# Two adjacency layers on one core: turning x and its weights with VectorE, moving leaky slopes to ScalarE and residual sums to GpSimd, and giving loads other queues

## The chip, the core and the metric

The kernel runs on one core of one Trainium2 chip. The core has TensorE (matrix products, shown as PE, with its weight loads as PEld), VectorE (DVE), ScalarE (ACT), GpSimd (POOL) and SyncE (SP), which here only issues transfers. SP, ACT and POOL each have a DMA queue of their own, and all queues share 16 DMA engines. The metric is the device time of one launch in microseconds (us). Before the change the median of three runs is 1766.97 us (1764.3 to 1770.71).

## The reference, cut to what is computed

The input x is 4096 x 512 (float32), adj is 4096 x 4096 (0 or 1, about 32 ones in a row).

```python
# layer 0
keep   = Ab & (cumsum(Ab, axis=1) <= 64)          # the first 64 neighbours of a row
cnt    = keep.sum(axis=1)
xj     = leaky_relu((keep @ X) / max(cnt, 1) @ W_nb.T + b_nb)     # slope 0.01
xi     = leaky_relu(X @ W_line.T + b_line)
x1     = layernorm(X + xi + where(cnt > 0, xj, 0))
# layer 1
Wh     = x1 @ W + bW
e      = leaky(Wh @ a1 + b1 + (Wh @ a2 + b2).T, 0.2); e = where(adj > 0, e, -9e15)
out    = layernorm(x1 + softmax(e, axis=1) @ Wh)
```

## The kernel before, in words

The 4096 rows are cut into 32 blocks of 128 rows (`NB`); a row block of x is 128 partitions by 512 columns (`C`). The product with W_nb is pulled in front of the aggregation: the kernel keeps Y = X @ W_nb.T in two halves (`y_hi`, `y_lo`, lines 344 and 373) and later multiplies the 0/1 map by both. There are four stages, each a Python loop whose order of calls is the order of the instructions on every engine; nothing reorders them.

**Stage 1, linear maps (loop at line 332).** For every block i TensorE makes two products of 4 x 2 matmul records (`linear`, line 288), with W_nb and with W_line. Both operands need the contraction on the partitions, so x and the weights must be turned first. `transpose_to` (lines 112 to 117) does this on TensorE: four 128 x 128 transposes into PSUM and one ScalarE copy out. `turn_x(i + 1)` stands at the head of iteration i. `own` (lines 317 to 322) is three VectorE operations (add the bias, `max(0.01 t, t)`, add x) and a store of `xi + x` to DRAM on the GpSimd queue. x is loaded once (`load_x`, line 238), on the ACT queue two blocks ahead. `fold_w` (line 300, at i = 2) works out W a1 and W a2 with ten VectorE operations.

**Flag chunks.** Beside the products the kernel turns adj into one byte per edge. A row block has two chunks of 2048 columns, 64 in all. `codes_until(s)` runs chunks until s of them are scanned; for each it issues `load_adj` (1 MB, SP queue, line 152), `edge` (ScalarE, line 158), `scan` (VectorE: a running count at line 169, a copy at 173, a product at 174, and for every fourth chunk five small operations, lines 182 to 186), and `pack` (ScalarE copy, line 192, store on the GpSimd queue, line 193). Tiles for chunks exist twice, so a load waits for the `edge` two chunks back. Before the change 22 chunks are made in stage 1.

**Stage 2, aggregation (loop at line 420).** For each block, 64 matmuls (line 433) add the map times `y_hi` and `y_lo`. The map comes back from DRAM turned by a DMA transpose (`load_kt`, line 387, two blocks ahead, SP queue) and is opened by ScalarE (`make_kt`, line 221). `finish(i - 1, g)` (line 389) finishes the block before in four pieces: scale, bias and leaky slope (394, 397), residual sum and statistics (401, 121 to 127; the power at line 127 runs on GpSimd), layer norm and store (132, 408), and two sums for the attention scores (413). The other 42 chunks are made here, 1.5 to a block.

**Stage 3, Wh = x1 @ W (loop at line 656).** x1 is loaded in squares of 32 partitions (`load_turned`, line 473, four transfers to a block, ACT queue, three blocks ahead), so that one VectorE instruction (line 491) that turns 32 x 32 squares turns the whole block. `load_ct(0)` (line 502) fetches four turned code blocks on the SP queue at i = 6. `greatest` (line 516, i = 12 to 19) takes the row maxima, with a ScalarE piece (523), a VectorE piece (527) and the next `load_nat` on SP. `shifts(0)` (line 534, i = 22) writes a small tile to DRAM and reads it back spread over the partitions (544, 546, SP queue).

**Stage 4, attention (loop at line 681).** `produce` makes the weights on ScalarE and VectorE, `consume` multiplies them by Wh (line 601).

Of the kernel before, what the change touches and what calls it, by code (L numbers as in the profile page):

```python
# [20 lines left out]
P = 128  # L21
SQ = 32
NEIGHBORS = 64.0
EPS = 1e-5

# [6 lines left out]
def two_layer_adj_gnn(  # L32
# [56 lines left out]
    bias_nb = const.tile([P, C], F32, name="bias_nb")  # L89

    wa = const.tile([P, 2, NC], F32, name="wa")
    wa_row = const.tile([P, 2, C], F32, name="wa_row")
# [45 lines left out]
    with ExitStack() as l0:  # L138
# [88 lines left out]
        with ExitStack() as la:  # L227
            wp = la.enter_context(tc.tile_pool(name="l0_w", bufs=1))
            work = la.enter_context(tc.tile_pool(name="l0_work", bufs=2))

            bias_line = wp.tile([P, C], F32, name="bias_line")
            w_t = {}
            xbs, xts, pys, pls = {}, {}, {}, {}

            def load_x(i):
                if i < NB:
                    xbs[i] = work.tile([P, C], F32, name="xb", bufs=4)
                    (nc.sync if i < 3 else nc.scalar).dma_start(xbs[i], x_blk(i))

            def turn_x(i):  # L240
                if i < NB:
                    xts[i] = work.tile([P, NC, P], F32, name="xt")
                    transpose_to(xts[i], lambda k: xbs[i][:, ts(k, P)], NC)
# [8 lines left out]
            for name in ("nb", "line"):  # L252
                t = early("a")
                raw[name] = [t[:, c, :] for c in range(NC)]
# [9 lines left out]
            def load_w(name, src, queues):  # L264
                for c in range(NC):
                    queues[c % len(queues)].dma_start(raw[name][c], src[ts(c, P), :])
# [7 lines left out]
            def turn_w(name, idle=0):  # L274

                wt = wp.tile([P, NC, C], F32, name=f"wt_{name}")
                for c in range(NC):
                    if idle:
                        spin(idle)
                    transpose_to(  # L280
                        wt[:, :, ts(c, P)], lambda k: raw[name][c][:, ts(k, P)], NC
                    )
# [28 lines left out]
            def spread_wa():  # L311
                nc.sync.dma_start(
# [4 lines left out]
            def own(i):  # L317
                t = work.tile([P, C], F32, name="t")
                nc.vector.tensor_tensor(t, pls.pop(i), bias_line, ALU.add)  # L319
                nc.vector.scalar_tensor_tensor(t, t, 0.01, t, ALU.mult, ALU.max)  # L320
                nc.vector.tensor_tensor(t, t, xbs.pop(i), ALU.add)
                nc.gpsimd.dma_start(own_d[i], t)

            load_x(0)
            load_w("nb", w_nb, (nc.scalar, nc.sync))
            load_x(1)
            load_w("line", w_line, (nc.sync,))
            load_x(2)
            spin(12)
            turn_x(0)  # L330
            turn_w("nb", 2)
            for i in range(NB):
                if i == 0:
                    nc.sync.dma_start(bias_line, b_line.partition_broadcast(P))
                if i > 0:
                    turn_x(i + 1)
                xt = xts.pop(i)
                pys[i] = linear(xt, "nb")
                if i == 0:
                    turn_w("line")  # L340
                pls[i] = linear(xt, "line")
                if i == 0:
                    turn_x(1)
                nc.scalar.copy(y_hi[:, i, :], pys[i])
                if i > 0:
                    own(i - 1)
                if i > 0:
                    load_x(i + 2)
                if i == 0:
                    load_w("w", w, (nc.sync,))  # L350
                if i == 1:
                    load_rows()
                    nc.gpsimd.dma_start(bias_nb, b_nb.partition_broadcast(P))
                if i == 2:
                    fold_w()
                if i == 3:
                    spread_wa()
                if i > 3:
                    codes_until(int((i - 3) * 22 / (NB - 6)) if i < NB - 3 else 22)
# [16 lines left out]
            own(NB - 1)  # L376
# [4 lines left out]
        RATE = 1.5  # L381
        start = done[0]

        def load_kt(b):
            if b < NB:
                ktbs[b] = ktb_p.tile([P, NT, P], BF16, name="ktb")
                nc.sync.dma_start_transpose(ktbs[b], code_d[b])

        def finish(i, g):
            if i < 0:  # L390
                return
            if g == 0:
# [4 lines left out]
                nc.vector.scalar_tensor_tensor(t, t, 0.01, t, ALU.mult, ALU.max)  # L397
                fin[i] = t
            elif g == 1:
                t, y = fin[i], owns.pop(i)  # L400
                nc.vector.scalar_tensor_tensor(
                    y, t, some[:, i : i + 1], y, ALU.mult, ALU.add
                )
# [365 lines left out]
```

## Time and profile before

The profiled execution took 1767.0 us, and its span (first to last instruction) is 1764.9 us; the other 2.1 us lie around it. It stands within 0.1 us of the median of the runs.

| stretch of the span, us | stage | PE busy, us | DVE busy, us | ACT busy, us |
|---|---|---|---|---|
| 0 to 67 | 1, start | 55.5 | 20.8 | 13.7 |
| 67 to 192 | 1 | 118.6 | 119.9 | 70.3 |
| 192 to 272 | 1, end | 77.6 | 78.0 | 42.2 |
| 272 to 736 | 2 | 464.0 | 407.1 | 297.2 |
| 736 to 870 | 3 | 118.0 | 86.2 | 25.8 |
| 870 to 1765 | 4 | 886.3 | 690.2 | 426.1 |

Busy time says that an engine had an instruction in it, not that the instruction ran at its best rate: matmuls are pipelined, and one that starts late can still be counted as busy. The chain of work that ended last, and the order of time of each engine, say which engine the others waited for. A queue name (SPq, ACTq) is time in which an engine's issuing part was busy or waited.

### The profile page before, as it was taken

What the parts mean: (1) busy time and instruction counts of PE and PEld (TensorE: products, weight loads), DVE (VectorE), ACT (ScalarE), POOL (GpSimd) and SP (SyncE); (2) the same over time, 40 slices, a digit from 0 to 9 for tenths busy, and PEclk for the clock granted to TensorE, in tenths of its full rate; (3) what the DMA queues carried; (4) which work ended last, traced back from release to release, by engine and by line L of the source; (5) the groups of instructions that cost most, each with busy time, mean ns of one, the idle gap of its engine ahead of it and who ended that gap; (6) DMA issues with size and microseconds to landing.
All of it is one profiled execution on the core that took longest, in us unless ns stands there. A gap on an engine that the chain in (4) does not pass through costs nothing.

```text
span 1764.9 us, 14748 instructions
## 1 busy us (share of the span) xinstructions
PE 1720.0 (97%) x5118; PEld 949.6 (54%) x5118; DVE 1402.2 (79%) x1649; ACT 875.3 (50%) x910; POOL 192.9 (11%) x234
## 2 busy tenths in 40 slices
PE   8799999999999999989899999999999999999998
PEld 5344447888888888733344444444444444444443
DVE  3599998999999997458677986968869689696754
ACT  2355555767667674112355463644636445364331
POOL 1011112223232322100000100001000010000100
PEclk9899999999999999999999999999999999999999
DMA  4566667676767673762402304122041220411100
GB/s 143 191 220 204 205 222 204 192 221 198 221 203 210 207 204 95 133 148 79 100 25 55 88 24 96 60 64 68 24 95 56 65 68 27 96 50 46 48 0 25
DMA packets 209227, 206.57 MB, mean 117 GB/s; under 512 B 154848, under 2 KB 170240, under 8 KB 200832
## 3 DMA queue, kind: packets, MB, share of 16 engines
q1 hardware_dynamic: 174352, 145.55, 30.8%
q0 software_dynamic: 13056, 44.07, 6.6%
q10 hardware_dynamic: 21744, 16.00, 3.4%
q8 instruction: 41, 0.67, 0.2%
q14 instruction: 34, 0.28, 0.1%
HBM read 130.02 MB, written 42.00 MB: 97 GB/s over the span
## 4 chain that ended last, share of the span: by engine, by line
PE 84%; DVE 8%; DMA 5%; issue 1%; SPq 1%; ACT 1%; ACTq 0%; POOLq 0%; DVEq 0%
PE acc L601 49%; PE acc L433 26%; PE acc L288 5%; DVE left L169 3%; PE acc L661 2%; DMA xb<-in_x_dram 2%; DMA ct<-code_d 1%; SPq L506 1%; PE pt L116 1%; DMA x1b<-x_d 1%; DVE pen L527 1%; DVE t L320 1%; DVE y_lo L373 1%; DMA uv_d<-uv 1%; DVE t L319 1%
## 5 line engine op out<-in xcount | busy, mean ns | idle before, releaser
L601 PE MATMUL acc<-wh,p 128*128 128x512 f32 x2048 | 881.2, 592 | 0.0
L601 PEld LDWEIGHTS acc<-wh,p 128*128 128x128 f32 x2048 | 388.5, 190 | 486.0 <-issue 485.3
L433 PE MATMUL acc<-y_lo,kt 128*128 128x512 f32 x1016 | 395.2, 389 | 0.0
L433 PE MATMUL acc<-y_hi,kt 128*128 128x512 f32 x1016 | 395.2, 389 | 0.0
L561 ACT ACTIVATE p<-row,e 128x512 f32<-128x512 f32 x256 | 182.8, 714 | 419.1 <-PE acc L601 367.4
L564 DVE TENSOR_TENSOR p<-p,p 128x1024 f32<-128x1024 f32 x128 | 156.2, 1221 | 124.7 <-ACT p L561 124.6
L127 POOL TENSOR_TENSOR rs<-ve,neg_half 128x1 f32<-128x1 f32 x64 | 101.5, 1587 | 1152.1 <-DVE ve L125 1152.1
L221 ACT ACTIVATE kt<-ktb,steep 128x1024 fp32r<-128x1024 uint8 x124 | 142.8, 1152 | 154.2 <-PE acc L433 154.2
L433 PEld LDWEIGHTS acc<-y_hi,kt 128*128 128x128 f32 x1016 | 190.8, 188 | 39.5
L433 PEld LDWEIGHTS acc<-y_lo,kt 128*128 128x128 f32 x1016 | 190.8, 188 | 39.5
L561 ACT ACTIVATE p<-row,e_fifth 128x512 f32<-128x512 f32 x256 | 180.8, 706 | 1.4 <-DVE p L564 1.3
L566 DVE TENSOR_TENSOR p<-p,ct 128x1024 f32<-128x1024 f32 x128 | 156.8, 1225 | 4.4
L523 ACT ACTIVATE pen<-nat,far 128x2048 bf16<-128x2048 uint8 x64 | 127.3, 1990 | 63.4 <-DMA x1b<-x_d 52.1
L571 DVE TENSOR_TENSOR zacc<-zacc,p 128x1024 f32<-128x1024 f32 x120 | 147.0, 1225 | 4.1
L169 DVE TENSOR_TENSOR_SCAN left<-two,edge 128x2048 bf16<-128x2048 f32 x32 | 141.4, 4417 | 6.4 <-ACT edge L158 6.4
L169 DVE TENSOR_TENSOR_SCAN left<-two,ends,edge 128x2048 bf16<-128x2048 f32 x32 | 143.3, 4478 | 0.0
L158 ACT ACTIVATE edge<-a,steep 128x2048 bf16<-128x2048 int32 x64 | 127.5, 1993 | 17.8 <-DVE left L174 10.5
L661 PE MATMUL acc<-ws,x_t 128*128 128x512 f32 x256 | 116.0, 611 | 16.0 <-DVE x_t L491 15.8
L192 ACT CAST code<-left 128x2048 uint8<-128x2048 bf16 x64 | 120.5, 1883 | 0.8 <-DVE left L174 0.8
L288 PE MATMUL acc<-wt_nb,xt 128*128 128x512 f32 x256 | 119.2, 610 | 0.9 <-ACT wt_nb L117 0.7
L288 PE MATMUL acc<-wt_line,xt 128*128 128x512 f32 x256 | 115.2, 592 | 0.7 <-ACT wt_line L117 0.7
L661 PEld LDWEIGHTS acc<-ws,x_t 128*128 128x128 f32 x256 | 49.1, 195 | 82.4 <-issue 57.0
(103 smaller groups left out, 1029.1 us busy)
## 6 DMA issues: line engine op xcount, KB each, us to landing
a<-in_adj_dram SPq DMA_DIRECT2D x64, 1024.0 KB, 5.5
code_d<-code POOLq DMA_DIRECT2D x64, 256.0 KB, 4.4
nat<-code_d SPq DMA_DIRECT2D x32, 512.0 KB, 3.6
own_d<-t POOLq DMA_DIRECT2D x32, 256.0 KB, 4.3
own<-own_d SPq DMA_DIRECT2D x32, 256.0 KB, 2.8
x_d<-own POOLq DMA_DIRECT2D x32, 256.0 KB, 3.4
x1b<-x_d SPq DMA_DIRECT2D x32, 256.0 KB, 5.5
x1b<-x_d ACTq DMA_DIRECT2D x120, 64.0 KB, 2.1
```

Source lines behind the costliest of these rows:

```text
L158: nc.scalar.activation(edge_of[s], loaded.pop(s), AF.Sigmoid, bias=steep[:, 0:1], scale=STEEP)
L169: nc.vector.tensor_tensor_scan(left, two.to_broadcast([P, CH]), e, NEIGHBORS + 2.0 if h == 0 else end, ALU.max, ALU.subtract,)
L221: nc.scalar.activation(kts[s], bytes_.rearrange("p t (i r) -> p t r i", r=2), AF.Sigmoid, bias=steep[:, 1:2], scale=STEEP,)
L288: nc.tensor.matmul(pl, lhs_t[:, k, :], w_t[name][:, k, :], start=(k == 0), stop=(k == NC - 1),)
L433: nc.tensor.matmul(accs[i], kt[:, k // 2, k % 2, :], term[:, j, :], start=(j == 0 and term is y_hi), stop=(j == NB - 1 and term is y_lo),)
L523: nc.scalar.activation(pen, nats[b].bitcast(U8)[:, ts(h, HALF)], AF.Relu, bias=far, scale=-FAR)
L561: nc.scalar.activation(dst[:, r, :], uvs[g][:, k, :], AF.Exp, bias=e[:, b : b + 1])
L564: nc.vector.tensor_tensor(p0, p0, p1, ALU.max)
L566: nc.vector.tensor_tensor(p0, p0, code.rearrange("p (x r) -> p r x", r=2), ALU.min)
L571: nc.vector.tensor_tensor(zaccs[g], zaccs[g], p0, ALU.add)
L601: nc.tensor.matmul(accs1[g][k], p_[:, r, ts(k, P)], wh[:, 2 * t_ + r, :], start=(t_ == 0 and r == 0), stop=(t_ == NT - 1 and r == 1),)
L661: nc.tensor.matmul(pw, x1t[:, k, :], ws[:, k, :], start=(k == 0), stop=(k == NC - 1))
```

## The change

- **x and the layer-0 weights are turned by VectorE.** They are loaded in squares (`squares`: four transfers of 64 KB to a block of x, eight of 128 KB to a weight), and `turn` is one VectorE transpose to a block of x and four to a weight. The TensorE transposes and the ScalarE copies of stage 1 go. The opening run of idle TensorE transposes (`spin`) grows from 12 (and 8 between weights) to 40.
- **x is loaded twice.** The squares come on the SP queue, three blocks ahead, into a constant tile `late` that later holds the bias and the attention rows. The plain copy for the residual sum comes on the GpSimd queue (`load_own_x`).
- **Leaky slopes go to ScalarE** (`AF.Prelu`) in stages 1 and 2; in stage 2 the factor `some` is applied there too. **Residual sums go to GpSimd** (`tensor_tensor` add).
- **20 chunks** are made in stage 1, and 44 in stage 2 at 25/16 to a block.
- **`finish`** has its sums (old line 413) one block later, and the statistics one piece later.
- **Stage 3:** `load_turned` moves from the ACT to the SP queue; `load_ct(0)` is issued one transfer at a time at i = 8, 11, 14 and 17. The bias and the spread rows come late, on the GpSimd queue (`load_late`).

```diff
+            AHEAD = 20
...
+            def squares(dst, src):
+                return [
+                    (dst[ts(n, SQ)], src[:, ts(n, P)].rearrange("(j a) c -> a j c", a=SQ))
+                    for n in range(NC)
+                ]
-            def load_x(i):
...
-                    (nc.sync if i < 3 else nc.scalar).dma_start(xbs[i], x_blk(i))
+            def load_turned_x(i):
+                if i < NB:
+                    xrs[i] = late[:, i % 3, :].rearrange("p (j c) -> p j c", c=P)
+                    for dst, src in squares(xrs[i], x_blk(i)):
+                        nc.sync.dma_start(dst, src)
+            def load_own_x(i):
+                xbs[i] = work.tile([P, C], F32, name="xb", bufs=4)
+                nc.gpsimd.dma_start(xbs[i], x_blk(i))
+            def turn(dst, src):
+                nc.vector.transpose(
+                    dst.rearrange("p m (j a) -> p j m a", a=SQ),
+                    src.rearrange("p j (m b) -> p j m b", b=SQ),
+                )
             def turn_x(i):
...
-                    transpose_to(xts[i], lambda k: xbs[i][:, ts(k, P)], NC)
+                    turn(xts[i], xrs.pop(i))
...
-            def own(i):
+            def own_line(i):
                 t = work.tile([P, C], F32, name="t")
                 nc.vector.tensor_tensor(t, pls.pop(i), bias_line, ALU.add)
-                nc.vector.scalar_tensor_tensor(t, t, 0.01, t, ALU.mult, ALU.max)
-                nc.vector.tensor_tensor(t, t, xbs.pop(i), ALU.add)
-                nc.gpsimd.dma_start(own_d[i], t)
+                return t
+            def own(i, t):
+                nc.scalar.activation(t, t, AF.Prelu, alpha=SLOPE)
+                y = xbs.pop(i)
+                nc.gpsimd.tensor_tensor(y, y, t, ALU.add)
+                nc.gpsimd.dma_start(own_d[i], y)
...
+            for k in (0, 1, 2, 3, 4, 5):
+                nc.scalar.dma_start(*nb_parts[k])
+            load_turned_x(0)
+            for k in (6, 7):
+                nc.sync.dma_start(*nb_parts[k])
+            load_turned_x(1)
+            for part in parts_of("line", w_line):
+                nc.sync.dma_start(*part)
+            load_turned_x(2)
+            spin(40)
             turn_x(0)
-            turn_w("nb", 2)
+            turn_w("nb")
+            turn_x(1)
+            turn_w("line")
             for i in range(NB):
...
+                load_turned_x(i + 3)
                 if i > 0:
                     turn_x(i + 1)
                 xt = xts.pop(i)
                 pys[i] = linear(xt, "nb")
                 pls[i] = linear(xt, "line")
                 nc.scalar.copy(y_hi[:, i, :], pys[i])
                 if i > 0:
-                    own(i - 1)
+                    t = own_line(i - 1)
...
                 if i == 2:
                     fold_w()
                 if i > 3:
-                    codes_until(int((i - 3) * 22 / (NB - 6)) if i < NB - 3 else 22)
+                    codes_until(min((i - 3) * AHEAD // (NB - 6), AHEAD))
...
                     y_lo[:, i, :], pys.pop(i), y_hi[:, i, :].bitcast(F32), ALU.subtract
                )
+                if i > 0:
+                    own(i - 1, t)
+                load_own_x(i)
+                if i == 1:
+                    load_rows()
+                if i == NB - 2:
+                    load_late()
...
-        RATE = 1.5
+        RATE = 25 / 16
         def finish(i, g):
+            if g == 0 and i > 0:
+                y, _ = fin.pop(i - 1)
+                for k in range(2):
...
+                        accum_out=e12[:, k, i - 1 : i],
             if g == 0:
...
-                nc.vector.scalar_tensor_tensor(t, t, 0.01, t, ALU.mult, ALU.max)
+                nc.scalar.activation(t, t, AF.Prelu, alpha=SLOPE, scale=some[:, i : i + 1])
             elif g == 1:
-                nc.vector.scalar_tensor_tensor(y, t, some[:, i : i + 1], y, ALU.mult, ALU.add)
+                nc.gpsimd.tensor_tensor(y, y, t, ALU.add)
+            elif g == 2:
                 fin[i] = y, ln_stats(y)
...
-                nc.scalar.dma_start(
+                nc.sync.dma_start(
...
-        if i == 6:
-            load_ct(0)
+        if i in range(8, 8 + 3 * GB, 3):
+            load_ct(0, (i - 8) // 3)
```

## The prediction, made before the changed kernel was run

> **What bounds the kernel now.** I read the page first: the busy times and the chain of work that ended last.
>
> ```profile
> PE 1720.0 (97%) x5118; PEld 949.6 (54%) x5118; DVE 1402.2 (79%) x1649; ACT 875.3 (50%) x910; POOL 192.9 (11%) x234
> PE acc L601 49%; PE acc L433 26%; PE acc L288 5%; DVE left L169 3%; PE acc L661 2%; DMA xb<-in_x_dram 2%; DMA ct<-code_d 1%; SPq L506 1%; PE pt L116 1%; DMA x1b<-x_d 1%; DVE pen L527 1%; DVE t L320 1%; DVE y_lo L373 1%; DMA uv_d<-uv 1%; DVE t L319 1%
> ```
>
> TensorE carries 84% of the chain, but the lines L433 and L601 (stages 2 and 4) hold nearly all of it. L288, the products of stage 1, has 5%, and VectorE lines stand beside it. So I asked for the busy times stage by stage (columns: stretch, its length, then busy us of PE, PEld, DVE, ACT, POOL, the granted clock, DMA share, GB/s):
>
> ```profile
> 67.00:192.00 125.00, 118.62 (x318) 54.11 (x317) 119.88 (x115) 70.25 (x60) 15.16 (x28) 0.99 0.64 214
> 272.00:736.00 464.00, 464.00 (x2049) 384.32 (x2048) 407.09 (x525) 297.19 (x211) 115.27 (x106) 1.00 0.67 193
> 736.00:790.00 54.00, 48.55 (x116) 21.30 (x115) 28.13 (x50) 5.08 (x4) 2.90 (x4) 0.97 0.79 160
> 830.00:870.00 40.00, 31.58 (x70) 13.51 (x69) 19.10 (x28) 8.74 (x14) 0.00 (x0) 0.91 0.53 110
> 870.00:1765.00 895.00, 886.33 (x2113) 395.85 (x2111) 690.24 (x752) 426.10 (x557) 42.44 (x60) 1.00 0.20 53
> ```
>
> In stage 1 (67 to 192) VectorE is busy 96%; stage 2 is solid TensorE; stage 3 has holes in every engine; stage 4 is TensorE again. The order of time on VectorE shows what one block of stage 1 costs:
>
> ```profile
> 84.07 0.68 DVE L373 TENSOR_TENSOR y_lo<-acc,y_hi 128x512 fp32r<-128x512 f32 x1
> 84.67 0.68 DVE L319 TENSOR_TENSOR t<-acc,bias_line 128x512 f32<-128x512 f32 x1
> 85.38 0.69 DVE L320 SCALAR_TENSOR_TENSOR t<-t 128x512 f32<-128x512 f32 x1
> 86.11 0.69 DVE L321 TENSOR_TENSOR t<-t,xb 128x512 f32<-128x512 f32 x1
> 86.72 4.42 DVE L169 TENSOR_TENSOR_SCAN left<-two,edge 128x2048 bf16<-128x2048 f32 x1
> ...
> 91.36 1.23 DVE L174 TENSOR_TENSOR left<-edge,left 128x2048 bf16<-128x2048 bf16 x1
> 92.50 0.69 DVE L373 TENSOR_TENSOR y_lo<-acc,y_hi 128x512 fp32r<-128x512 f32 x1
> ```
>
> From start to start: y_lo 0.60, bias 0.71, slope 0.73, sum 0.61, chunk 5.78, in all 8.43 us a block, while the two products take TensorE 6.87 (their groups start at 261.56, 264.99 and 268.42). VectorE sets the pace. The chain in order of time shows the holes of stage 3, which runs from 737.4 to 869.15, 131.8 us for 32 x 3.43 = 109.9 of products, so 21.9 are lost:
>
> ```profile
> 745.08 11.87 DMA ct<-code_d
> 757.81 6.71 DMA x1b<-x_d
> ...
> 829.01 9.22 DMA uv_d<-uv
> ...
> 847.54 5.73 DMA ct<-code_d
> ```
>
> Loads of x1 wait behind four DMA transposes at 742 to 765 and again at 838 to 858. I put the loss at 6.3 us for the first (idle 3.8 before 755.17, then 10.2 us for 18 records worth 7.7), 10.7 for the second (27.9 us from 841.25 for five blocks of 3.43) and the rest, 4.9, at `greatest`, where VectorE needs 4.18 a block.
>
> **Stage 1, the steps.** *Start.* Before, block 1 begins at 22.03. Now the 40 idle transposes end at 10.8 at the rate of the first twelve (2.82 us for 12), or about 8 at the later rate (0.60 for four). SP issues 4 + 2 + 4 + 8 + 4 transfers at some 0.44 each (the median of L474, the same form): x0 is out by 2.5, line's weights by 8.9; ACT's six parts of nb by 3.4. With 4 to 5 us to landing (nb now: 4.6 to 4.9) and four transposes of 0.71 (L491), the first product starts near 10; line's weights are turned near 14.5, and block 1 starts near 18.0: 4 us earlier.
>
> *VectorE per block.* Slope (0.73) and sum (0.61) go, a turn comes at 0.71 (L491, 709 ns, the same shape). A block has 0.71 + 0.71 + 0.60 = 2.02, with a chunk 7.80. The formula puts 20 chunks in blocks 5 to 29: 25 x 2.02 + 20 x 5.78 + 5 x 0.9 (the small operations) = 170.6, against 25 x 6.87 = 171.8 on TensorE. They balance, and single blocks may be late: a turn may start when TensorE ends block i - 1 (two `xt` tiles) and is needed one block later, so 6.87 - 0.71, about 6 us, are free. The old TensorE transposes (0.43 a block) and copies (0.58 on ACT) go. Two chunks (11.6) move to stage 2.
>
> *ScalarE.* y_hi 0.59, edge 1.99, pack 1.88 and the slope, taken as an ACTIVATE of 128x512 (L561, 0.71): 5.2 us a block, under 6.87. It is behind edge and pack; who waits for it is GpSimd's add alone. Relu (L523) ran after Sigmoid in stage 3 without a table load, so I take none for Prelu.
>
> *GpSimd.* The add has no row. Bounds: 0.3 us (a one-input 128x128 operation at the start, 0.295) and 4.67 (the power L127 beside a scan); four times 0.295, 1.18, is nearest in size and is my value. What it does to VectorE is the open cost:
>
> ```profile
> L127 POOL TENSOR_TENSOR rs<-ve,neg_half x64: 549/720/4667, 290.1 to 1758.8; 128x1 f32<-128x1 f32 x64
> ```
>
> ```profile
> 583.09 4.48 DVE L169 TENSOR_TENSOR_SCAN left<-two,ends,edge 128x2048 bf16<-128x2048 f32 x1
> ...
> 583.32 4.60 POOL L127 TENSOR_TENSOR rs<-ve,neg_half 128x1 f32<-128x1 f32 x1 [8.14 <-DVE ve L125]
> ```
>
> The first fence is the operation's shortest, median and longest time, the second a meeting: GpSimd's 0.56 us become 4.60 when a scan began first. No scan in the trace is longer than 4.48, so VectorE never paid, for an operation of one column. A block costs VectorE 0 (these rows) to 1.18 (it waits the add out). The add comes after pack, near TensorE's block start plus 8.6, when the next scan starts at 8.3 plus VectorE's lateness: it meets a scan most often and then holds up the product behind it. I take 0.8 a chunk: 20 x 0.8 - 6 = 10 us; ends 0 and 20 x 1.18 - 6 = 17.6. The Trainium skill (SBUF — State Buffer, "Who interferes with whom") speaks against the change here: a two-input VectorE operation and a GpSimd operation that reads SBUF exclude each other for their whole length. The meeting above agrees (0.56 became 4.60). By the page the block pays the whole add, 17.6 us and a total of 1737; by the rows alone 0 and 1719.
>
> *Queues.* On GpSimd the own x load (0.54 to issue) and store stand behind the add, so the code store of the next chunk does too; the load of x is used one block later (3.2 us to landing), 7 us off. On SP the squares stand before `load_adj`, which waits for an edge one block back; they are needed three blocks later: 10 us are free by these rows, so nothing (were it gone, about what late x loads cost TensorE now, 17.0 us in 14 waits). The bias and spread rows come at block 30, two blocks ahead of use, against 6.7 to 6.9 us to landing: nothing. `fold_w` now waits for rows issued behind the first add (landing near 31.5); it ends at 39, and the turn for block 4, due at 38.6, comes at 40.7: 2.2 us.
>
> Stage 1 ends at 18.0 + 31 x 6.87 + 2.2 + 10 = 243.2 instead of 272.0: **-28.8 us**.
>
> **Stage 2.** VectorE has 14.5 us a block now and is late at times (block 27's L394 starts at 685.2 against 678.4). It loses L397 and L401 (1.51) and gains 0.0625 x 5.78 = 0.36. The add returns some of it: when a chunk stands between L394 and the statistics (78% of blocks), 1.0; when none does, VectorE waits for slope and add, 2.2; mean 1.3. That gives 14.65 against 14.5, 4.6 us late by block 29. The last map's load is issued at 693.5 and wanted near 714, which leaves 14 us of cover: **0**. Were each add to cost 2.0, VectorE would be 25 us late: +11. ScalarE has 4 x 1.15 + 1.56 x 3.87 + 0.71 = 11.4.
>
> **Stage 3.** The four code transfers come singly, SP has issued x1 three blocks ahead (10 us, against 6 us for one transpose's landing), so 6.3 becomes 0.7 (the last block's finish now runs over ACT and GpSimd, some 1.7 us longer). At i = 22 x1's loads stand behind SP's wait for `uv_d` (9.2 us): block 26's lands 16 us after block 23 began, is due at 10.3, so 6.5 idle plus 1.7 at a low clock (0.91 above): 8.2 instead of 10.7. `greatest` 4.0 instead of 4.9, as ACT no longer issues x1. Sum **-9.0**; ends -17 (all but 4.9 gone) and 0. Stage 4 has no edit: 0.
>
> **Sum:** 1767.0 - 28.8 - 9.0 = **1729 us**; the profiled execution stands at the median of the runs.
>
> **Rivals.**
> - *Something other than TensorE still sets stage 1.* Its bytes rise to 23 (adj) + 17 (x twice) + 8.4 + 5.2 + 4.4 = 58 MB. At the highest rate of any slice, 222 GB/s, that is 261 us, so 11 saved and 9 in stage 3: 1747. For it: x loads already took up to 9.64 us; against: the DMA share is 0.64. VectorE kept at 8.43 a chunk gives nearly the same: 272 less two chunks, 260.
> - *Slower: stage 2 waits for GpSimd's add.* If statistics wait behind an add that waits behind a scan, a block costs VectorE 13.35 + 4.67 + 1.18 = 19.2, so 4.7 over 14.5 x 29 = 136, less 14 of cover: 1851. It decides from where the gain (38) and the cover (14) are eaten, 52 / 29 = 1.8 over 14.5, that is 2.9 to 3.0 us an add. Against: VectorE has a chunk to do in between in most blocks.
> - *Prelu reloads tables.* By L158's load row (1.28), two a block: 7.8 on ACT in stage 1, 20 x 0.9 = 18 us more, 1747; stage 2 13.9, hidden.
>
> The Trainium skill (ScalarE: Activation LUTs, "What ACT_TABLE_LOAD costs") puts a switch at 2.66 us with its drain; no run here shows the drain, and by that figure stage 2 would need 16.7 a block, some 70 us more.
>
> **How the numbers follow.** The sum 62% (1712 to 1740), the first rival 20% (1740 to 1760), tables 5%, stage 2 on GpSimd 8%, gain eaten by chance 5%. Low end: no add cost (-10), no fold wait (-2), stage 3 better by 5: 1712. High end: add at 1.18 (+7.6), stage 2 at +11, stage 3 at nothing (+9), 1757, and the first rival: 1760. Faster 0.86, within 0.3% (what a measurement of this kernel can tell from no change) 0.03, slower 0.11.
>
> **What would show it.** Right: block 1 near 18, L433 from about 243, blocks of 6.9 without VectorE in the chain; code transfers one by one; a hole of 6 to 8 us after `shifts`. Wrong: adds of over 3 us with idle before the statistics; table loads beside the slopes; squares late at the turns; L433 with holes.

## The result: 0.4% slower, and where the time went

The changed kernel takes 1774.3 us in the median of 16 executions (1762.0 to 1781.9), the kernel before 1766.7 on the same chip (1762.8 to 1770.7). The ratio is 1.0037, with a 95% interval of 1.0021 to 1.0052: slightly slower, where 1729 us had been predicted, with 1760 as the high end. The profiled execution of the changed kernel took 1769.8 us with a span of 1768.0, so it stands below its median; the kernel before had a span of 1764.9.

The stage ends of the two profiled executions, and of the runs further down, are the first products of the next stage (for stage 3 the first transpose of x1). All are us of the profile; the last column counts from the first product of stage 4 to the end of the span.

| kernel | stage 1 ends | stage 2 takes | stage 3 takes | stage 4 and end | span |
|---|---|---|---|---|---|
| before | 271.5 | 464.6 | 132.9 | 895.9 | 1764.9 |
| predicted for the change | 243.2 | 464.6 | 123.9 | 895.9 | 1727.1 |
| changed | 259.3 | 483.3 | 126.4 | 898.9 | 1768.0 |
| e1 own x ahead | 253.0 | 468.0 | 125.7 | 898.6 | 1745.3 |
| e12 own x on SP | 251.0 | 469.3 | 127.6 | 896.0 | 1743.9 |
| e3 old finish | 264.4 | 481.5 | 124.5 | 898.6 | 1769.0 |
| e4 stage 3 only | 269.2 | 464.7 | 124.8 | 895.9 | 1754.6 |
| e8 e1 + late store | 246.5 | 468.1 | 126.2 | 898.6 | 1739.4 |
| e13 all, warm start | 239.9 | 468.0 | 126.8 | 898.5 | 1733.2 |
| e14 e13, own x on SP | 234.0 | 469.4 | 125.5 | 896.1 | 1725.0 |

Against the prediction the change misses 16.1 us in stage 1, 18.7 in stage 2, 2.5 in stage 3 and 3.0 at the very end; with the half microsecond by which the prediction had rounded stage 1's old end (272.0 for 271.5, so that its row adds up to 1727.6), that is, but for rounding, the 40.9 between 1727.1 and 1768.0. Stage 1 gained 12.1, stage 3 6.5, and stage 2 gave it all back.

### The profile page after: what moved, and what is told of

Same layout as the page of the kernel before. It is cut to its first block, busy times and chain, and to the rows that moved or that the text cites. A ratio compares the mean times of both kernels' runs of the same rounds, so it can differ in the third digit from the quotient of the medians.

```text
span 1768.0 us, 14554 instructions
## 1 busy us (share of the span) xinstructions
PE 1706.8 (97%) x4978; PEld 936.0 (53%) x4978; DVE 1355.4 (77%) x1561; ACT 886.1 (50%) x934; POOL 329.9 (19%) x331
## 4 chain that ended last, share of the span: by engine, by line
PE 68%; DMA 11%; DVE 8%; POOL 6%; issue 4%; ACT 1%; SPq 1%; POOLq 0%; ACTq 0%; DVEq 0%
PE acc L642 49%; PE acc L473 14%; DMA xb<-in_x_dram 8%; POOL xb L351 3%; PE acc L702 3%; DVE left L172 3%; DVE left L177 1%; POOL own_d L352 1%; DMA uv_d<-uv 1%; DVE pen L568 1%; DVE junk L431 1%; POOL own L448 1%; DMA a<-in_L_gnn_W_nb_dram 1%; POOL rs L130 1%; SPq L515 0%
## 5 line engine op out<-in xcount | busy, mean ns | idle before, releaser
L473 PE MATMUL acc<-y_hi,kt 128*128 128x512 f32 x1016 | 398.2, 392 | 12.9 <-ACT kt L224 12.8
L130 POOL TENSOR_TENSOR rs<-ve,neg_half 128x1 f32<-128x1 f32 x64 | 85.4, 1334 | 964.7 <-DVE ve L128 964.7
L602 ACT ACTIVATE p<-row,e_fifth 128x512 f32<-128x512 f32 x256 | 180.8, 706 | 18.7 <-DVE p L605 18.7
L224 ACT ACTIVATE kt<-ktb,steep 128x1024 fp32r<-128x1024 uint8 x124 | 137.4, 1143 | 32.5 <-PE acc L473 23.3
L313 PEld LDWEIGHTS acc<-wt_nb,xt 128*128 128x128 f32 x256 | 49.2, 196 | 91.0 <-issue 57.6
```

The source lines that it names most:

```text
L224: nc.scalar.activation(kts[s], bytes_.rearrange("p t (i r) -> p t r i", r=2), AF.Sigmoid, bias=steep[:, 1:2], scale=STEEP,)
L313: nc.tensor.matmul(pl, lhs_t[:, k, :], w_t[name][:, k, :], start=(k == 0), stop=(k == NC - 1),)
L473: nc.tensor.matmul(accs[i], kt[:, k // 2, k % 2, :], term[:, j, :], start=(j == 0 and term is y_hi), stop=(j == NB - 1 and term is y_lo),)
L602: nc.scalar.activation(dst[:, r, :], uvs[g][:, k, :], AF.Exp, bias=e[:, b : b + 1])
```

## The profile after

First the busy times and, below them, the chain of work that ended last, by line.

```profile
PE 1706.8 (97%) x4978; PEld 936.0 (53%) x4978; DVE 1355.4 (77%) x1561; ACT 886.1 (50%) x934; POOL 329.9 (19%) x331
...
PE acc L642 49%; PE acc L473 14%; DMA xb<-in_x_dram 8%; POOL xb L351 3%; PE acc L702 3%; DVE left L172 3%; DVE left L177 1%; POOL own_d L352 1%; DMA uv_d<-uv 1%; DVE pen L568 1%; DVE junk L431 1%; POOL own L448 1%; DMA a<-in_L_gnn_W_nb_dram 1%; POOL rs L130 1%; SPq L515 0%
```

Before, the products of stage 2 carried 26% of the chain; now 14%. In their place stands a transfer that the prediction had at no cost, the load of own x (`xb<-in_x_dram`, 8%), with the GpSimd sum that uses it (L351, 3%). The busy times by stage, with the columns of the table before (length, then PE, PEld, DVE, ACT, POOL, clock, DMA share, GB/s):

```profile
67.00:192.00 125.00, 111.05 (x248) 47.59 (x249) 111.46 (x104) 64.47 (x58) 55.93 (x58) 0.96 0.72 233
259.30:742.70 483.40, 470.52 (x2051) 385.06 (x2050) 382.77 (x467) 319.57 (x247) 184.15 (x148) 0.99 0.68 194
742.70:790.00 47.30, 45.96 (x114) 20.83 (x113) 26.43 (x48) 5.58 (x5) 4.16 (x5) 1.00 0.66 158
830.00:870.00 40.00, 31.44 (x70) 13.54 (x69) 19.70 (x29) 8.18 (x13) 0.00 (x0) 0.91 0.50 119
870.00:1768.00 898.00, 886.45 (x2113) 395.97 (x2111) 689.75 (x751) 425.28 (x556) 42.24 (x60) 1.00 0.20 53
```

In stage 1 (first row) VectorE did get lighter, 111.5 of 125 us instead of 119.9, but TensorE is busy less too, 111.1 instead of 118.6: something else sets the pace. Stage 2 (second row) is no longer solid TensorE: 470.5 of 483.4, so 12.9 us of its loss are holes; the rest of the 18.7 is longer busy time (464.6 before), at a granted clock of 0.97 between 259 and 300 us. The waits of GpSimd (engine and line, what it waited for, us in total, times, longest) name the something:

```profile
POOL xb L351 <- DMA xb<-in_x_dram: 114.8, 27, 11.0
...
POOL xb L351 <- ACT t L349: 43.3, 4, 25.7
```

27 of the 32 sums wait for their own x. The order of time in the middle of stage 1 shows why (start, duration, engine, line; in brackets the idle time before it and what ended it):

```profile
147.41 0.54 POOL L254 DMA_DIRECT2D xb<-in_x_dram  x1
...
151.98 2.28 POOL L351 TENSOR_TENSOR xb<-xb,t 128x512 f32<-128x512 f32 x1 [3.48 <-DMA xb<-in_x_dram]
...
154.55 0.56 POOL L352 DMA_DIRECT2D own_d<-xb  x1 [0.30 <-POOL xb L351]
...
155.11 0.54 POOL L254 DMA_DIRECT2D xb<-in_x_dram  x1
...
160.03 1.26 POOL L351 TENSOR_TENSOR xb<-xb,t 128x512 f32<-128x512 f32 x1 [3.85 <-DMA xb<-in_x_dram]
161.33 0.69 DVE L345 TENSOR_TENSOR t<-acc,bias_line 128x512 f32<-128x512 f32 x1 [5.13 <-POOL xb L351]
...
161.59 0.56 POOL L352 DMA_DIRECT2D own_d<-xb  x1 [0.30 <-POOL xb L351]
162.14 0.54 POOL L254 DMA_DIRECT2D xb<-in_x_dram  x1
```

Sum, 0.3 us, store issued, load issued, landing, next sum: the load for the next block is issued only when the sum of this one is over, and the next sum needs that load. It is a ring with one transfer in flight. From the sum at 104.48 to the one at 260.98 it goes round 21 times in 156.5 us, 7.45 us a round, against the 6.87 that TensorE needs for a block. VectorE is drawn in at 161.33: the tile `t` has two buffers, and VectorE waits 5.13 us for GpSimd to free one, with the turn of the next x in line behind.

A second loss stands at the start of the chunks:

```profile
62.24 1.28 ACT L161 ACT_TABLE_LOAD   x1 [6.79 <-DMA a<-in_adj_dram]
...
65.57 4.42 DVE L172 TENSOR_TENSOR_SCAN left<-two,edge 128x2048 bf16<-128x2048 f32 x1 [8.85 <-ACT edge L161]
...
72.65 0.70 DVE L258 STREAM_TRANSPOSE xt<-late 128x512 f32<-128x512 f32 x1
...
73.40 2.07 PE L313 MATMUL acc<-wt_nb,xt 128*128 128x512 f32 x2 [8.28 <-DVE xt L258]
```

VectorE waits 8.85 us for the first edge, that is for the first adjacency, and as the turn of x is now a VectorE instruction behind the scan, TensorE stands for 8.28 us. The queue of SP shows why the adjacency is late:

```profile
41.35 0.41 SPq L334 DMA_DIRECT2D wa_d<-wa  x1
41.80 13.99 SPq L250 DMA_DIRECT2D late<-in_x_dram  x12
55.84 10.04 SPq L155 DMA_DIRECT2D a<-in_adj_dram  x3
```

From 27.0 to 41.35 SP issues nothing: the store of the folded weights `wa_d` (L334) waits 14.3 us for VectorE's folding, with the x squares of three blocks and then the adjacency behind it.

## The experiments

### e1: own x loaded ahead of the sum

```diff
-                if i > 0:
-                    own(i - 1, t)
-                load_own_x(i)
+                if i == 0:
+                    load_own_x(0)
+                load_own_x(i + 1)
+                if i > 0:
+                    own(i - 1, t)
```

> The changed kernel, with the own x of a block loaded one block earlier and issued on GpSimd's queue ahead of the residual sum instead of behind it. Bytes, engines and sums stay. Theory A (in stage 1 GpSimd runs a loop of its own: sum 1.4 us, store issue 0.56, load issue 0.54, landing 3.3 to 11.4, next sum; this loop and not TensorE sets the pace): the waits of GpSimd's sum for its x (114.8 us in 27 times) go; stage 1 ends near 248 us (my 243.2 plus the 5.0 us by which block 1 began later than I had put it) instead of 259.3, and the hole of 6.5 us at the start of stage 2 shrinks too, since it hangs on the last of these loads: 1755 to 1764 us. Rival B (VectorE loses time to the GpSimd sums that it meets): the loop goes, but blocks stay over 7.5 us on VectorE, stage 1 ends at 255 or later, 1768 or more. Rival C (the transfers set stage 1, 233 to 243 GB/s): x lands as late as before whenever it is issued, stage 1 ends at 257 to 261, 1774 as it is.

1747.4 us (1746.9 to 1748.9), ratio to the kernel before 0.9903 (0.9888 to 0.9918): 17 us faster than before and, by the two ratios, some 24 faster than the changed kernel. The waits of GpSimd for x are gone; it now waits for ScalarE:

```profile
POOL code_d L196 <- ACT code L195: 182.6, 54, 6.3
...
POOL xb L352 <- ACT t L350: 64.5, 13, 26.3
```

Theory A holds, and was too small: stage 1 ends 6.3 us earlier, and stage 2 returns from 483.3 to 468.0, of which I had expected only a part. Rival C falls, since the same bytes now flow at 254 GB/s between 67 and 192 us instead of 233; rival B's sign, an end of stage 1 at 255 or later, did not come either (253.0, not the 248 of theory A). What is left above 248 is not the price of the sums: e8, with the same sums, ends stage 1 at 246.5. The ring did most of its harm after stage 1. At its end GpSimd was behind, and the start of stage 2 hung on its last round. Changed kernel, waits of ScalarE in 259 to 300 us, and under them those of SP:

```profile
ACT edge L161 <- DMA a<-in_adj_dram: 10.1, 1, 10.1
ACT kt L224 <- DMA ktb<-code_d: 9.1, 1, 9.1
```

```profile
SPq L468 <- DMA own_d<-xb: 13.1, 1, 13.1
```

SP waits 13.1 us to read back the own rows of a block that GpSimd has not yet summed; the adjacency and the maps stand behind this on SP, ScalarE waits for them, and TensorE has a hole of 6.47 us at 299.46. With own x ahead, TensorE's waits for the maps in stage 2 go from 12.8 us in 8 times to 2.1 in 2.

### e12: the same place in the program, another queue

```diff
-                nc.gpsimd.dma_start(xbs[i], x_blk(i))
+                nc.sync.dma_start(xbs[i], x_blk(i))
```

> The changed kernel with one edit: the load of own x stays at its place in the program and is issued on the queue of SP instead of GpSimd's. Theory A in its narrow form (the load stands behind the sum on GpSimd's own queue, so that load and sum wait for each other in turn): the load no longer waits for a sum, GpSimd's waits for x (114.8 us in 27 times) go, 1747 to 1755, near the first experiment. If the short lead of one block is what counts, since the load lands 3 to 11 us after its issue: waits of GpSimd for x remain at half or more, 1762 to 1772. If SP's own waits (for an edge before each adjacency load) hold it up as much: 1770 or more.

1746.5 us (1745.6 to 1747.9), ratio 0.9882 (0.9866 to 0.9899). The place in the program is that of the changed kernel, landings are no shorter (median 5.0 us against 4.6), and the gain is that of e1: GpSimd's waits for x fall from 114.8 us in 27 times to 18.4 in one. So it is the place behind the sum on GpSimd's own queue, as theory A has it in its narrow form, and not the short lead in the program.

### e3 and e5: stage 2's end of a block as before

```diff
-                nc.scalar.activation(
-                    t, t, AF.Prelu, alpha=SLOPE, scale=some[:, i : i + 1]
-                )
+                nc.vector.scalar_tensor_tensor(t, t, SLOPE, t, ALU.mult, ALU.max)
...
-                nc.gpsimd.tensor_tensor(y, y, t, ALU.add)
-                fin[i] = y
+                nc.vector.scalar_tensor_tensor(
+                    y, t, some[:, i : i + 1], y, ALU.mult, ALU.add
+                )
+                fin[i] = y, ln_stats(y)
```

> The changed kernel, with the end of a block of stage 2 as the kernel before has it (slope, residual sum and row sums on VectorE, statistics one quarter earlier), the rest as changed; the rate of code chunks in stage 2 stays at 25/16. Rival D (the residual sum on GpSimd makes the statistics late, and this lengthens stage 2 from 464 to 483 us): stage 2 returns to about 466 and the time falls by 15 to 19, to 1755 to 1759. Theory A (stage 2 loses at its start only, through what is still pending of stage 1's loads and stores on GpSimd): the holes at 264 to 300 us stay, stage 2 at 478 or more, 1769 to 1775.

1771.0 us, ratio 1.0041 (1.0028 to 1.0054), against 1.0037 for the changed kernel: no difference, and stage 2 still takes 481.5. Rival D falls. With own x ahead as well (e5):

> Both edits in one kernel: own x ahead of the sum in stage 1, and the end of a block of stage 2 on VectorE as before. Theory A alone: as with the first edit alone, 1755 to 1764. Rival D alone: as with the old end alone, 1755 to 1759. If both causes are at work and do not overlap, the gains add up: stage 1 ends near 248 and stage 2 takes about 466, which gives 1740 to 1748.

1750.2 us, ratio 0.9915 (0.9902 to 0.9929); e1 on the same chip had 0.9903 (0.9888 to 0.9918). Nothing adds up: the end of the block on ScalarE and GpSimd costs nothing that these runs can tell. If anything it saves a little: the four runs of e5 (1749.0 to 1750.6) all lie above the four of e1 (1746.9 to 1748.9), and stage 2 takes 470.9 against 468.0.

### e4: only stage 3 changed, in the kernel before

```diff
-                nc.scalar.dma_start(
+                nc.sync.dma_start(
                     x1rs[i][ts(n, SQ)].rearrange("a j m b -> a j (m b)"),
...
-        if i == 6:
-            load_ct(0)
+        if i in range(8, 8 + 3 * GB, 3):
+            load_ct(0, (i - 8) // 3)
```

> The kernel before, with only the third stage changed: loads of x1 on the queue of SP, the transposed loads of the codes one by one every third block. My step of the prediction: -9.0 us, so 1758. By the changed kernel's trace, where the stage took 126 us against 131.8: -6, so 1761. Rival: the stage's gain is eaten by the wait behind the shifts, 0.

1755.9 us (1754.6 to 1756.8), ratio 0.9948 (0.9935 to 0.9960), that is 9.2 us by the ratio. The stage takes 124.8 instead of 132.9, 8.1 less. This step of the prediction, -9.0, stands.

### e2: the sum of stage 1 on VectorE, own x ahead

```diff
-                nc.gpsimd.tensor_tensor(y, y, t, ALU.add)
+                nc.vector.tensor_tensor(y, y, t, ALU.add)
```

> The changed kernel with own x loaded ahead (the first experiment, 1747.4 us), and the residual sum of stage 1 on VectorE again; slope, turning and stage 2 stay as changed. This prices the sum on GpSimd. My step: a sum on GpSimd costs VectorE 0.8 us a chunk, on VectorE it costs 0.61 to 0.69 a block. In the first experiment's trace the products that a sum meets take 1.92 instead of 1.23 and scans 4.52 to 4.93 instead of 4.42, about 0.7 to 0.9 a chunk. By that, 25 x 0.65 = 16 us more on VectorE against 20 x 0.8 = 16 less: 1745 to 1750, no difference. Rival E (what the sum on GpSimd costs VectorE is the shadow of other waits, VectorE does not set stage 1): also no difference, but products at 1.92 remain. Rival F (GpSimd's sums cost VectorE more than they save, by the whole length of 1.26 and more): faster than the first experiment by 8 or more, 1739 or less. If the sums cost next to nothing: slower by up to 16, 1763.

1751.9 us, ratio 0.9908 (0.9895 to 0.9922), against 0.9903 for e1: no difference by the ratios, as expected. Rival F falls, and so does a sum that costs next to nothing. Rival E's sign is absent too: in e2 all products of stage 1 take 1.22 to 1.23. In this kernel VectorE's 25 sums and the shadow of GpSimd's come to the same.

### e6a and e6: the first adjacency and edge earlier

```diff
+                if i == 2:
+                    load_adj(0)
+                    load_adj(1)
+                if i == 3:
+                    edge(0)
```

> The changed kernel with one edit: the first two loads of the adjacency are issued three blocks earlier and the first edge two blocks earlier, so that the first scan does not wait for them. Theory G (VectorE's wait of 8.8 us in front of the first scan holds up the turn of block 7's x and with it TensorE: 8.28 us idle and then eight products at 0.80 each instead of 0.43, 2.7 us): up to 11 us off where TensorE sets the pace, 1763. Theory A (GpSimd's loop sets the rest of stage 1 anyway, and swallows what is won here, as it runs at its own pace of 7.3 to 9.6 us a block): 1770 to 1774, no difference beyond 4 us.

1780.5 us, ratio 1.0068 (1.0055 to 1.0081): slower than the changed kernel, which neither theory had. The loads I moved still stood behind the store of the folded weights (issued at 42.21), and the edge that I moved now made ScalarE wait in front of other work. Why this costs time here and not in e6 below, which has the same edit, no run shows.

```profile
58.06 1.28 ACT L161 ACT_TABLE_LOAD   x1 [16.72 <-DMA a<-in_adj_dram]
...
62.38 0.69 DVE L402 TENSOR_TENSOR y_lo<-acc,y_hi 128x512 fp32r<-128x512 f32 x1 [15.40 <-ACT y_hi L374]
```

> Both edits: own x ahead of the sum, and the first adjacency loads and edge earlier. Theory G: the hole at 66 to 74 us of the first experiment (7.84 us and 3 us at a low clock) goes, and with the loop gone nothing swallows it: 1747.4 - 8 to 11 = 1736 to 1739. Rival: VectorE at 123.6 busy of 125 us sets stage 1 by itself, and the chunks start no earlier because the adjacency is late anyhow: 1745 to 1748.

With own x ahead: 1748.9 us, ratio 0.9888 (0.9874 to 0.9902), no difference from e1. I had taken the moment of the issue for the cause; the cause was what the issue stood behind.

### e8 and e10: the store of the folded weights four blocks later

```diff
                 nc.vector.tensor_tensor(ca, ca, b12, ALU.add)
+
+            def store_wa():
                 nc.sync.dma_start(wa_d.rearrange("k (c p) -> p k c", p=P), wa)
...
                 if i == 2:
                     fold_w()
+                if i == 6:
+                    store_wa()
```

> The first experiment (own x ahead, 1747.4 us) with one more edit: the store of the folded weights (wa_d) is issued on SP four blocks later. In the changed kernel SP waits from 27.0 to 41.35 us for VectorE's folding before that store can go, with the x squares of blocks 5 to 7 and the first adjacency loads behind it; 12 squares then take 14 us, the adjacency is issued at 55.84 and the first edge starts near 64. Theory H (this wait on SP's queue is the cause of the hole of 7.8 us at 66 to 74 us, and of the eight products at 0.8 us behind it): the squares go out at 27 to 35, the adjacency at the turn of block 5, near 50, and the hole shrinks to under 2 us: 1737 to 1741. Rival I (the adjacency lands late because 1 MB takes 6 us whenever it is issued at block 5, and VectorE waits in line): the hole stays at 6 to 8 us, 1746 to 1748.

On top of e1: 1741.6 us (1741.0 to 1742.3), ratio 0.9870 (0.9857 to 0.9884), below e1's interval. Stage 1 ends at 246.5 instead of 253.0, and TensorE's longest wait for a turn falls from 7.8 us to 1.5. Theory H holds, with a gain just under what I gave it (1737 to 1741).

> The changed kernel with the later store alone, own x still loaded behind the sum. Theory H with theory A (GpSimd's loop of sum, store, load and landing sets the pace after the hole and swallows what is won before it): the hole shrinks, stage 1 ends within 3 us of 259 all the same, 1770 to 1778. If the hole counts in full beside the loop: 1774 - 8 to 11 = 1763 to 1766.

In the changed kernel alone: 1768.8 us, ratio 1.0027 (1.0018 to 1.0036), against 1.0037 (1.0021 to 1.0052): not told apart, and 1.2 us below the range of theories H and A. Stage 1 ends at 262.2. As those theories together have it, the ring swallows what the later store wins.

### e7 and e9: the order at the start, and all edits

```diff
-            load_turned_x(1)
             for part in parts_of("line", w_line):
                 nc.sync.dma_start(*part)
+            load_turned_x(1)
             load_turned_x(2)
```

In addition `line` is turned before x of block 1, and own x of blocks 0 and 1 is loaded on SP at block 0 instead of at the very start on GpSimd.

> As the kernel with both edits, and the start in another order: x of blocks 1 and 2 behind the weights of line, own x of blocks 0 and 1 behind them on SP instead of at the very start on GpSimd. My step: the first product near 10 and block 1 near 18.0; they came at 13.81 and 23.02, and at 15.82 and about 24.6 with own x ahead, while the 16 transfer engines were busy 0.89 to 0.95 of the first 23 us. If the order of the transfers makes the start late: the first product at 11 to 12.5, block 1 at 19 to 21, 3 to 5 us less than the kernel with both edits (1736 to 1739 expected there), so 1732 to 1736. Rival: the 512-byte pieces of the weights themselves take the time; no difference beyond 2 us.

1745.8 us, ratio 0.9875 (0.9859 to 0.9890). The first product comes at 13.46 instead of 15.40 and block 1 at 21.91 instead of 24.60, but by the ratios the time is not told apart from the kernel without this edit (0.9888). The runs lean to the first theory: on the same chip the four of e7 (1744.8 to 1746.5) lie below the four of e6 (1746.6 to 1749.6), 3.0 us in the median. With the late store too, and the edge at block 4 (e9):

> All edits so far: own x ahead, the start in the other order, the first adjacency loads issued at block 2, the first edge at block 4 (at block 3 it stood on ScalarE in front of y_hi for 15 us in the last two kernels), and the store of the folded weights four blocks later. Theory H: no hole at 60 to 75 us, block 1 at 21 to 22, stage 1 ends at 240 to 243: 1745.8 - 8 to 11 = 1735 to 1738. Rival I: 1743 to 1747.

1740.3 us, ratio 0.9865 (0.9850 to 0.9880). Less than expected, and not told apart from e8: two holes were left. At the start TensorE is idle for 5.43 us before its first product, and the folding, in one go, holds the turn up; after each hole eight products take 6.74 and 5.39 us instead of 3.60.

### e13: idle transposes up to the first product, folding spread

```diff
-            spin(40)
+            spin(70)
...
-                if i == 2:
-                    fold_w()
+                if i == 3:
+                    fold_w((0, 1, 2))
+                if i == 4:
+                    fold_w((3, 4))
```

> The kernel with all edits (1740.3 us), with 70 idle transposes at the start instead of 40 and the folding of the weights spread over blocks 3 and 4 instead of in one go at block 2. In that kernel's trace TensorE is idle for 5.43 us before the first product, and the first eight products then take 6.74 us instead of 3.60; the folding leaves it idle for 2.66 us, and eight products behind it take 5.39. If idle time ahead of a product is what makes it slow: 3 us less at the start and 4 us less at the folding, 1733 to 1737. If the start is bound by the landing of the weights and the lateness of VectorE is only moved: 1738 to 1741.

1734.6 us (1733.4 to 1735.2), ratio 0.9812 (0.9797 to 0.9826). Stage 1 ends at 239.9, 3.3 us before the 243.2 of the prediction. The first product of e9 and its product behind the folding, and then the first product of e13:

```profile
13.75 6.74 PE L310 MATMUL acc<-wt_nb,xt 128*128 128x512 f32 x8 [5.43 <-DVE wt_nb L255]
...
47.19 5.39 PE L310 MATMUL acc<-wt_nb,xt 128*128 128x512 f32 x8 [2.66 <-DVE xt L255]
```

```profile
13.59 3.70 PE L310 MATMUL acc<-wt_nb,xt 128*128 128x512 f32 x8 [1.63 <-DVE wt_nb L255]
```

The weights arrive no earlier; the products alone are faster, because TensorE was kept busy until they came. Rows first: after 5.43 us of idle time eight products took 6.74 us, after 1.63 us 3.70; between 13 and 21 us the granted clock is 0.57 in e9 and 1.00 in e13. The Trainium skill (TensorE: Matmul & The Clock Gate, "What's actually happening") says that the clock falls to half after an idle window of about 3.4 us. The first products agree; but in e9 the gap of 2.66 us at the folding was also followed by eight products at 5.39 us (granted clock 0.68 between 47.1 and 52.5), so here less than 3.4 us was enough.

### e14: own x on SP in the best kernel

```diff
-                    (nc.sync if i < 2 else nc.gpsimd).dma_start(xbs[i], x_blk(i))
+                    nc.sync.dma_start(xbs[i], x_blk(i))
```

> The best kernel so far (1734.6 us) with all loads of own x on SP's queue instead of GpSimd's, one block ahead as there. If these loads on GpSimd's queue cause the 2.6 to 3.0 us behind the last recorded instruction: the stretch falls from 7.6 to about 5 us, 1731.5 to 1732.5 if stage 1 keeps its end at 239.9. If SP's waits in front of the adjacency loads hold the loads of x up, stage 1 ends later by a few us and eats the gain: 1733 to 1738. If the stretch has another cause: it stays at 7.6.

1726.9 us (1726.7 to 1728.0), ratio 0.9789 (0.9776 to 0.9803): 2.1% faster than the kernel before, the best of all. The stretch behind the last recorded instruction falls to 5.1 us, as expected, and stage 1 ends 5.9 us earlier, which I had not expected. TensorE's waits for a turn fall from 4.1 us to 1.1; why the queue of these loads changes that stays open. Its two stretches of stage 1:

```profile
67.00:192.00 125.00, 123.88 (x290) 54.64 (x289) 119.63 (x115) 72.33 (x64) 45.66 (x50) 1.00 0.81 270
192.00:234.00 42.00, 42.00 (x100) 18.56 (x99) 37.09 (x37) 23.21 (x22) 15.55 (x19) 1.00 0.74 233
```

TensorE is busy 165.9 of 167 us here. From block 1 at 20.16 to the end at 234.0 a block takes 6.90 us, the 6.87 of the products alone but for 0.03.

## Why the prediction was wrong

**The step that failed is the one on the queues.** It said that on GpSimd the own x load and the store stand behind the add, that the load is used one block later and lands in 3.2 us, "7 us off", and so cost 0. I had counted the time to the use from the place in the program, but the queue is in order: the issue waits for the sum before it, and the sum waits for the load before that. What I took for 7 us of cover was the length of the ring itself: 1.3 to 3.4 for the sum, 0.3, 0.56 for the store's issue, and 3.4 to 7.5 from the load's issue to the next sum, 7.45 us a round in the middle. Seeing the ring would not have been enough: with my 1.18 for the sum and 3.2 for the landing it takes 5.2 us, under TensorE's 6.87. On average the two came to 1.7 and 4.9. By the ratios, e1 and e12 price this step at 24 and 27 us of the 45. The 27 hold the 2.9 us at the very end that e12 saves beside the ring (896.0 against 898.9 in the table).

**The same step, SP's half, also failed.** "10 us are free by these rows, so nothing" was counted for the squares before `load_adj`, and the store of the folded weights was not counted on SP's queue at all; `fold_w` was priced by the turn behind it alone, at 2.2 us. The turn did come only 0.48 us late (TensorE's wait at 44.26). But the store held SP for 14.3 us, and the hole behind it is 8.28 us and eight products at 6.39 instead of 3.70. e8 wins 5.8 us by moving it.

**The start** was mis-sized. I had block 1 at 18.0, it came at 23.0. I put each issue at 0.44 us; the six parts of nb took ScalarE's queue 8.53 us to issue, and four squares on SP 5.14. The first product waited 5.05 us for nb's weights, which were turned from 10.90 on, and then ran at half speed for four products. e13 gets block 1 to 21.5 and e14 to 20.2, so no run reached 18.

**The pace of stage 1**, VectorE's 7.80 a chunk block in balance with TensorE's 6.87 a block, was right. e13 and e14 show it: with both queues clear TensorE sets the pace, and the sums on GpSimd take nothing from it. The 10 us that I had put down for them were too many. Their price on VectorE itself was about right in e13: the product beside them, in the changed kernel's stage 1 mostly 1.23, has a median of 1.92 there, by 0.7 longer, and the longest scan grows from 4.48 to 5.90. It is no fixed price: in e14, with the same sums, the median is 1.23 again. In e1, where VectorE was busy 123.6 of 125 us, that counted; e2 shows it worth as much as VectorE's own sum. In my sum it was a cost of the path, and there the slack of 6 us a block covers it.

```profile
L177 DVE TENSOR_TENSOR left<-edge,left x19: 1224/1919/2742, 71.0 to 245.8; 128x2048 bf16<-128x2048 bf16 x19
```

That row is e13's between 67 and 259 us (shortest, median and longest ns); before, all 64 took 1224 to 1227. The Trainium skill (SBUF — State Buffer, "Who interferes with whom") says that the two engines lock each other out for a whole instruction, and that the order of issue decides who waits. The direction agrees in part: e13's product at 94.00 us, behind a sum that began at 92.62, takes 1.92, and GpSimd's sum, 1.26 alone, took up to 5.46. But the longest product (2.74, at 220.11) is recorded 0.37 us ahead of its sum (1.28, at 220.48), so the recorded starts do not always show who began first. That the median price of 0.7 is below the whole sum would fit a sum that had partly run when the product came up.

**Stage 2: 0** was right for its own edits (e3, e5) and wrong for what stage 1 handed over: 15.3 of the 18.7 us go with the ring. The other 3.4 remain in e1 and in e13 (468.0), with TensorE's waits for maps at 2.1 us; e5, with the slopes back on VectorE, does not take them away (470.9), so their cause stays open.

**Stage 3: -9.0** was right (e4). In the changed kernel it is -6.5: 1.1 us go to the end of stage 2's last block over ScalarE, ahead of the first copy of stage 3, as the step had it in part. The hole behind `shifts`, which I had put at 8.2, is TensorE's longest wait in the stage, 8.6, and stands in the chain:

```profile
829.24 11.61 DMA uv_d<-uv
842.68 3.09 DMA x1b<-x_d
...
846.62 22.66 PE acc L702 x48
```

**The rivals.** The first one, that transfers set stage 1 at 222 GB/s with its end at 261, looks confirmed by the 259.3 that came out. It is not: e14 ends at 234.0 with the same bytes at up to 270 GB/s. Of the slower side I had only the wait of the statistics for GpSimd's sum, with 2.9 us a sum as its point; e3 excludes it. GpSimd did decide, through its queue and not its arithmetic. Table loads fall: slopes take 0.63 us in stage 1 and have none beside them.

## What to carry to other kernels

A load that is moved onto the queue of the engine that consumes it, behind that consumption, makes a ring with one transfer in flight; its length is the sum, the store's issue and the time from the load's issue to its landing under load, and it is compared with the block's time before the load is called free. For every instruction that waits on a queue, list what stands behind it there until the wait is over: here a store that nobody needs for 28 blocks cost 5.8 us. When an operation moves to an engine that can wait for something else, TensorE inherits that wait, as with the turns behind the first scan.

## What the runs showed that I had not expected

The span ends 5.0 us after the last recorded instruction of a compute engine in the kernel before and in e4, and 5.1 in e12 and e14, but 7.6 to 8.0 in the changed kernel, e1, e3 and e13. The former have no loads of x on GpSimd's queue, the latter have. These rows of the changed kernel and of e14, whose spans are 1768.0 and 1725.0, read:

```profile
1759.48 0.55 DVE L135 TENSOR_SCALAR y<-y,mv,rs 128x512 f32<-128x512 f32 x1 [0.73 <-POOL rs L130]
```

```profile
1719.31 0.55 DVE L135 TENSOR_SCALAR y<-y,mv,rs 128x512 f32<-128x512 f32 x1 [0.73 <-POOL rs L130]
```

What happens in these 2.6 to 3 us the profile does not show; that the queue of these loads causes them is shown by e14, where nothing else differs from e13.

The changed kernel's time is also the least certain: its 16 executions lie between 1762.0 and 1781.9, 19.9 us apart, the 16 of the kernel before within 7.9, four of e1 within 2.1 and five of e14 within 1.3. The landing time of the one transfer in flight (3.3 to 11.4 us) could go into such a time, but that the ring is the cause is not shown: e10 has the same ring, and its 11 executions lie within 4.7 us.
